# A layer stack of attention, feed-forward and Mamba-2 mixer on one core: the mixer's opening, the place of B and C, of the inner products and of the last weights

## The chip, the core and the metric

The kernel runs on one core of one Trainium2 chip. A core has five engines with a queue each, and each queue runs in order: TensorE (PE) for matmuls, VectorE (DVE), ScalarE (ACT), GpSimd (POOL), and SyncE (SP), which here only starts DMA transfers. The metric is the device time of one execution in microseconds; what is compared is the median of several executions.

## What is computed

Input x is 4 sequences of 256 tokens with 512 channels, all in float32. Four layers follow one another, each added to its input: attention with an adapter, a clustered feed-forward layer, the mixer (a Mamba-2 layer with 128 heads of 64, state size 128, 8 groups), and the feed-forward layer again. The change is in the mixer alone:

```python
x = x + attn_a(layernorm(x)); x = x + ffn(layernorm(x))
x = x + attn_b(layernorm(x)); x = x + ffn(layernorm(x))
# attn_b, the mixer:
proj = input_states @ in_proj_w.T
gate, xBC, dt = proj[..., :8192], proj[..., 8192:18432], proj[..., 18432:]
xBC = silu(causal_conv4(xBC) + conv_b)
hs, Bm, Cm = ...                        # x by head; B and C by group
dt = softplus(dt + dt_bias); dA = dt * A
y = ssd(hs, A, Bm, Cm, D, dt)           # sum over j <= i of (C_i.B_j) exp(sum of dA over j+1..i) dt_j x_j, plus D x
g = y * silu(gate)
gg = g.reshape(b, l, G, GS)             # normalised by group of 1024 channels
g = (gg * rsqrt(mean(gg * gg) + EPS)).reshape(b, l, INTER) * norm_w
return g @ out_w.T
```

## The kernel before

**Tiling.** Tokens lie in one row of 1024 (`NT`), in two halves of 512, in chunks of 64 (`Q`), or in eight tiles of 128 (`TT`). The 8192 inner channels are 64 blocks (`NB`) of 128 channels, two heads each; eight blocks (`GB`) are a group, which has one B and one C block of its own. Products in float32 precision are made by `mm3` (L110): both operands are split into an upper and a lower part and three matmuls are summed. So every weight is first cast (upper part, ACT) and then subtracted (lower part, DVE or POOL). `upper_piece(i)` (L821) makes the upper part of projection weight i and gives back a function that makes the lower part and fetches weight i+3; `upper_out(n)` (L1163) does it for an output weight, scaled by the norm weight.

**Projection.** `projected(kind, n)` (L1243) is a generator: the first `next` allocates a PSUM tile `pp` for 128 channels x 1024 tokens, each further one issues 12 matmuls for one half of the tokens. Two such tiles exist (`ps_p`); only the gate of block 0 lies in another place. A tile is free again when its last reader is done: for x, B and C the three `taps` on DVE (L1000), for a gate its Silu on ACT.

**A block i** (L1323) works with three generations of data: it projects x and gate of block i, and finishes block i-1:

- `decays(i-1)`: `exponentials` (L1073) on ACT for both heads, 7 activations each, on tiles `em` which `differences` (L1061, DVE) filled;
- `turn(i-1)`: 8 transposes `trx` on PE, multiplied by dt on DVE (L1102);
- `weigh(i-1)`: the `em` tiles times the masked scores `gm` of the group, on DVE (L1092);
- `conv` (ACT, L989) and `taps` (DVE) on x of block i, then `side_by_side` (Silu on ACT, L1015);
- `inner_products(i-1)`: 32 products `pyy` on PE (L1118, 64 records in the trace), then `gated` on DVE (L1125), which frees the PSUM of `pyy` and gives gb;
- `spilled` writes gb of block i-2 to DRAM, `squared` (L1143) adds its square to the group's `sq`: Square on ACT, addition on POOL (DVE for block 63);
- the gate's Silu `gts[i]` (L1442) at the end.

Beside this, from group 1 on, a block makes the output product `outer` of one token tile of the group before (24 matmuls `pog`); the gated values come back from DRAM by `recall` and are split by `upper_recalled` (L1205). B of the next group is projected at the end of a group's fourth block, C at the end of its fifth (`NEXT`), and the block after applies `conv`, `taps` and Silu to it. The seventh block of a group makes the next group's `scores` (L1024), in four parts `pg`, two PSUM tiles at a time.

**Opening.** The weights dt and B are projected before the mixer's block loop. `steps()` (L925) is a generator on dt: step 1 adds the bias; step 2 takes softplus by exp and log, with a polynomial e(1 - e/2 + e^2/3) where e is small; step 3 scales and makes cumulated sums of both halves (`tensor_tensor_scan`), stores them to DRAM (`cumd`), and step 4 transposes them (`trd`). `rows(h)` (L1048) loads a head's cumulated sums back, broadcast to 64 partitions, as `r`. `started()` (L1261) runs steps 1 to 3 around B and C, and blocks 0 and 1 follow as cases of `block`: block 0 runs step 4, block 1 makes the scores of group 0 between projection of x and turn.

**Order.** In the mixer's loop the order on PE, ACT, DVE and POOL is the program's (`tc.manual_schedule`, L1461); the order of SP's transfers and of what follows the loop is the scheduler's. In block 63 the last `outer` and four `upper_out` come, and `begin(0)`, `begin(1)`, `begin(2)`, which recall and split gated values of the last group, all ahead of the gate's Silu. After the loop (L1467 to L1486) come decays, turn and weigh of block 63, three half output products `begun`, the last inner products, and the sums of squares `pqs`; then the final loop over the eight token tiles (L1503) with output products, norm and feed-forward.

Of the kernel before, what the change touches and what calls it, by code (L numbers as in the profile page):

```python
# [20 lines left out]
P = 128  # L21
B, L, C = 4, 256, 512
NT = B * L
# [56 lines left out]
def hybrid_kernel(  # L80
# [705 lines left out]
    def mixer(feed, later):  # L786
        with ExitStack() as es, ExitStack() as inner:
# [137 lines left out]
            def steps():  # L925

                reset = p2.tile([P, NT], F32, name="reset", tag="sq", bufs=1)[:, :512]
# [7 lines left out]
                for e in es2:  # L935
                    nc.scalar.activation(e, e, AF.Exp)
                for e, lg in zip(es2, lgs):
                    nc.scalar.activation(lg, e, AF.Ln, bias=ones[:, 0:1])

                for s, e, engine in zip(ss, es2, (nc.vector, nc.gpsimd)):  # L940
                    engine.tensor_scalar(s, e, 1.0 / 3.0, -0.5, ALU.mult, ALU.add)
                    engine.tensor_tensor(s, s, e, ALU.mult)
                    engine.tensor_scalar(s, s, 1.0, None, ALU.add)
                    engine.tensor_tensor(s, s, e, ALU.mult)
# [20 lines left out]
                yield  # L965
# [7 lines left out]
                yield  # L973
# [169 lines left out]
            def squared(n, x2, gb):  # L1143

                g = n // GB
                if g not in sqs:
                    sqs[g] = p2.tile([P, NT], F32, name="sq", tag="sq", bufs=1)
                    nc.scalar.activation(sqs[g], gb, AF.Square)
                else:
                    nc.scalar.activation(x2, gb, AF.Square)  # L1150
                    (nc.gpsimd if n < NB - 1 else nc.vector).tensor_tensor(sqs[g], sqs[g], x2, ALU.add)  # L1151
# [6 lines left out]
            def fetch_out(n):  # L1158
                if n < NB:
                    wraws[n] = po_.tile([P, C], F32, name="wor", tag="wor", bufs=4)  # L1160
                    load(wraws[n], wout[n])

            def upper_out(n):  # L1163

                r = wraws.pop(n)
                w = [po_.tile([P, C], F32R, name=f"wo{j}", tag=f"wo{j}", bufs=GB) for j in range(2)]
                wos.setdefault(n // GB, []).append(w)
                nc.scalar.activation(w[0], r, AF.Copy, scale=nw_s[:, n : n + 1])

                def lower():  # L1170
                    nc.vector.scalar_tensor_tensor(
                        w[1], r, nw_s[:, n : n + 1], w[0].bitcast(F32), ALU.mult, ALU.subtract
                    )
                    if n % GB < 4:
                        fetch_out(n + 4)

                return lower
# [83 lines left out]
            def started():  # L1261

                prepare(2)
                next(dt_steps)
                pieces.pop(0)
                group["b"] = conv(first[1], NB, False)
                taps(group["b"], first[1], NB)
                next(dt_steps)
                prepare(3)
                fetch(6)  # L1270
                pp = whole(projected("c", 0))
                group["c"] = conv(pp, NB + G, False)
                silu(group["b"])
                next(dt_steps)
                taps(group["c"], pp, NB + G)
                rr.update((h, rows(h)) for h in range(2))

# [29 lines left out]

            def decays(i):
                for h, e in zip((2 * i, 2 * i + 1), ems[i]):
                    exponentials(h, e)  # L1310
# [8 lines left out]
            def inner_products(i):  # L1319
                py = product(xds.pop(i), ems.pop(i))  # L1320
                gbs[i] = gated(i, xs2[i], gts.pop(i), py)

            def block(i):  # L1323
# [33 lines left out]
                if i:  # L1357
                    decays(i - 1)
                waiting = [k for k in "bc" if k + "pp" in group]
                for k in waiting:  # L1360
                    group[k] = conv(group[k + "pp"], (NB if k == "b" else NB + G) + g + 1, False)
                if i == 1:
                    next(x_steps)
                    scoring = scores(group.pop("b"), group.pop("c"))
                    gms[0] = next(scoring)
                    for _ in scoring:
                        pass
                if i:
# [18 lines left out]
                if i == 0:  # L1387
                    pp = whole(g_steps)
                    next(dt_steps)
                    silu(group["c"])  # L1390
# [50 lines left out]
                gts[i] = p2.tile([P, NT], F32, name="gt", tag="gt", bufs=2)  # L1441
                nc.scalar.activation(gts[i], pp, AF.Silu)  # L1442
# [42 lines left out]
            rgs[G - 1] = root(sums(G - 1))  # L1485
            nc.vector.reciprocal(rgs[G - 1], rgs[G - 1])  # L1486
# [110 lines left out]
```

## Time and profile before

| | us |
|---|---|
| median of 3 executions (1876.27 to 1877.36) | 1876.93 |
| the profiled execution | 1875.91 |
| its span, first to last instruction | 1874.1 |
| PE busy | 1792.8 |
| DVE busy | 1428.6 |
| ACT busy | 1275.4 |
| POOL busy | 252.1 |

The mixer's normalisation begins at about 363 us, C's projection at 390 us; in block 7, the last of group 0, the Silu of x starts at 555.68 us; block 63 is under way at 1748 us, and the final loop runs from about 1800 us. An operation's row in the profile names line, engine, operation, output and inputs, and its duration. A number in brackets behind it is the time for which the engine stood idle before it, with what released it. The page also gives, in 40 slices of 46.9 us, the busy share of each engine and the clock granted to PE in tenths of full speed. Durations of PE are modelled and overlap: two matmuls of 512 columns that follow one another show 0.39 us each, and start 0.2275 us apart.

The larger transfers, with the engine that issues them and the median time from issue to landing:

```profile
wr<-in_win_dram SPq DMA_DIRECT2D x144, 256.0 KB, 2.7
r<-cumd SPq DMA_DIRECT2D x256, 128.0 KB, 2.9
gr<-spill SPq DMA_DIRECT2D x120, 256.0 KB, 3.3
wor<-in_wout_dram SPq DMA_DIRECT2D x64, 256.0 KB, 4.3
```

### The profile page before, as it was taken

The numbers are of one execution on the slowest core, as the hardware profiler recorded it, in microseconds if no ns is written. First come the engines' busy times: TensorE is split into PE (matmuls) and PEld (weight loads), VectorE is DVE, ScalarE is ACT, GpSimd is POOL, SyncE is SP. The second block draws the span as 40 slices with busy tenths as digits, with TensorE's granted clock in tenths as the row PEclk, the third lists the DMA queues.
The fourth block names the chain that finished last, engine by engine and source line by source line (L and its number), as shares of the span: only waits on it lengthen the run. The fifth ranks groups of instructions, "written<-read, shape, count | busy, mean of one in ns | idle before, by whom it ended". The sixth has DMA issues, their size and how long they took to land.

```text
span 1874.1 us, 33084 instructions
## 1 busy us (share of the span) xinstructions
PE 1792.8 (96%) x12882; PEld 1463.0 (78%) x12882; DVE 1428.6 (76%) x2156; ACT 1275.4 (68%) x2518; POOL 252.1 (13%) x255
## 2 busy tenths in 40 slices
PE   8999988889799999999999999999999999999997
PEld 6777767677677888888888888888888888888776
DVE  5576667777788787877787887879787878887776
ACT  6666675366678666766776677668676866777653
POOL 6332230010111011011110110111111011101100
PEclk9999989889999999999999999999999999999999
DMA  4000000112225332533343243224332532343321
GB/s 144 1 1 1 22 15 24 42 45 80 84 85 158 96 96 85 158 107 96 113 130 102 91 150 120 86 96 147 96 101 86 172 105 92 112 134 108 101 82 50
DMA packets 134237, 169.45 MB, mean 90 GB/s; under 512 B 12224, under 2 KB 77376, under 8 KB 134080
## 3 DMA queue, kind: packets, MB, share of 16 engines
q1 hardware_dynamic: 125008, 134.30, 23.6%
q10 hardware_dynamic: 9072, 33.03, 4.6%
q8 instruction: 101, 1.65, 0.3%
q14 instruction: 56, 0.46, 0.1%
HBM read 131.64 MB, written 35.65 MB: 89 GB/s over the span
## 4 chain that ended last, share of the span: by engine, by line
PE 80%; DVE 8%; ACT 7%; issue 2%; POOL 1%; DMA 1%; SPq 0%; DVEq 0%; ACTq 0%; POOLq 0%
PE pp L115 14%; PE pp L117 13%; PE pp L116 13%; PE pyy L1118 8%; PE pog L115 6%; PE pog L117 6%; PE pog L116 6%; PE trx L1099 3%; ACT e L477 2%; PE ptr L493 1%; PE pq L115 1%; PE pg L1036 1%; DVE acc L1006 1%; PE pq L116 1%; PE pq L117 1%
## 5 line engine op out<-in xcount | busy, mean ns | idle before, releaser
L115 PE MATMUL pp<-mx,w 128*128 128x512 f32 (+1 forms) x1160 | 468.2, 404 | 10.3 <-DVE bc L1006 9.8
L117 PE MATMUL pp<-mx,w 128*128 128x512 f32 (+1 forms) x1160 | 455.0, 392 | 1.9 <-DVE w L830 1.9
L116 PE MATMUL pp<-mx,w 128*128 128x512 f32 (+1 forms) x1160 | 454.8, 392 | 0.0
L1151 POOL TENSOR_TENSOR sq<-sq,x 128x1024 f32<-128x1024 f32 x55 | 132.0, 2399 | 1257.5 <-ACT x L1150 1257.5
L115 PEld LDWEIGHTS pp<-mx,w 128*128 128x128 f32 x1160 | 220.2, 190 | 56.8 <-issue 10.6
L117 PEld LDWEIGHTS pp<-mx,w 128*128 128x128 f32 x1160 | 220.2, 190 | 48.9 <-DVE w L830 2.6
L116 PEld LDWEIGHTS pp<-mx,w 128*128 128x128 f32 x1160 | 220.8, 190 | 40.7
L1006 DVE SCALAR_TENSOR_TENSOR acc<-pp,cw_s,acc 128x1012 f32<-128x1012 f32 (+2 forms) x192 | 244.6, 1274 | 7.2 <-ACT acc L995 2.6
L1092 DVE TENSOR_TENSOR em<-em,gm 128x1280 f32<-128x1280 f32 x128 | 188.7, 1489 | 70.8 <-ACT em L1087 70.8
L1102 DVE TENSOR_TENSOR xd<-trx,dt_t 128x512 f32<-128x512 f32 x128 | 82.5, 686 | 168.8 <-PE trx L1099 168.8
L115 PE MATMUL pog<-wo,gh 128*128 128x512 f32 x512 | 202.3, 395 | 2.3 <-ACT gh L1209 1.3
L117 PE MATMUL pog<-wo,gh 128*128 128x512 f32 x512 | 200.8, 392 | 0.8 <-DVE gh L1214 0.8
L116 PE MATMUL pog<-wo,gh 128*128 128x512 f32 x512 | 200.3, 392 | 0.0
L1018 ACT ACT_TABLE_LOAD x63 | 80.8, 1283 | 163.4 <-DVE acc L1006 163.3
L1442 ACT ACTIVATE gt<-pp 128x1024 f32<-128x1024 f32 x64 | 65.7, 1027 | 161.8 <-PE pp L117 161.8
L1118 PEld LDWEIGHTS pyy<-em,xd 64*64 64x64 f32 x4096 | 136.1, 136 | 50.7 <-issue 17.6
L1118 PE MATMUL pyy<-em,xd 64*64 64x256 f32 (+3 forms) x4096 | 164.6, 306 | 7.8 <-DVE em L1092 7.8
L1079 ACT ACTIVATE em<-r,end_t 128x128 f32<-128x128 f32 x512 | 163.0, 389 | 0.8
L477 ACT ACTIVATE e<-sc,nmx 128x256 f32<-128x256 f32 (+1 forms) x256 | 104.0, 441 | 21.0 <-DVE nmx L471 20.9
L115 PEld LDWEIGHTS pog<-wo,gh 128*128 128x128 f32 x512 | 96.8, 189 | 22.8 <-ACT gh L1209 1.8
L117 PEld LDWEIGHTS pog<-wo,gh 128*128 128x128 f32 x512 | 96.7, 189 | 21.4 <-DVE gh L1214 1.1
L116 PEld LDWEIGHTS pog<-wo,gh 128*128 128x128 f32 x512 | 96.8, 189 | 19.5
(298 smaller groups left out, 3191.3 us busy)
## 6 DMA issues: line engine op xcount, KB each, us to landing
wr<-in_win_dram SPq DMA_DIRECT2D x144, 256.0 KB, 2.7
r<-cumd SPq DMA_DIRECT2D x256, 128.0 KB, 2.9
spill<-gb ACTq DMA_DIRECT2D x63, 512.0 KB, 3.2
gr<-spill SPq DMA_DIRECT2D x120, 256.0 KB, 3.3
wor<-in_wout_dram SPq DMA_DIRECT2D x64, 256.0 KB, 4.3
out_dram<-x SPq DMA_DIRECT2D x8, 256.0 KB, 2.4
x<-in_x_dram SPq DMA_DIRECT2D x1, 1536.0 KB, 8.8
gr<-spill SPq DMA_DIRECT2D x8, 192.0 KB, 2.5
```

The costliest lines, as they stand in the source:

```text
L115: nc.tensor.matmul(o, lh, rh, start=(first and k == 0), stop=False)
L116: nc.tensor.matmul(o, lh, rl, start=False, stop=False)
L117: nc.tensor.matmul(o, ll, rh, start=False, stop=(last and k == n - 1))
L477: nc.scalar.activation(es_[c][:, 2 * j + pr, :], sc[:, j, :], AF.Exp, bias=nm[:, j : j + 1], accum_out=rs[:, c, h : h + 1],)
L1006: nc.vector.scalar_tensor_tensor(av[:, :, d:], pv[:, :, : L - d], cw_s[:, ch, tap : tap + 1], av[:, :, d:], ALU.mult, ALU.add,)
L1018: nc.scalar.activation(pair(x2).rearrange("p k u i -> p u k i"), acc.rearrange("p (u k i) -> p u k i", u=2, i=Q), AF.Silu,)
L1079: nc.scalar.activation(piece(e, j, c, 2 - c, 2), rv[:, j, 2:, :], AF.Exp, bias=end_t[:, 2 * j + c, h : h + 1],)
L1092: nc.vector.tensor_tensor(e, e, gm, ALU.mult)
L1102: nc.vector.tensor_tensor(xd[:, hs, :].rearrange("p c (h d) -> p c h d", h=2), tr.rearrange("p c (h d) -> p c h d", h=2), dt_t[:, hs, 2 * ...
L1118: nc.tensor.matmul(py[d, u, j * L + c * Q : (j + 1) * L].rearrange("p (k i) -> p k i", i=Q), xd[us, 4 * j + c, d], piece(es2[hh], j, c)[us ...
L1151: (nc.gpsimd if n < NB - 1 else nc.vector).tensor_tensor(sqs[g], sqs[g], x2, ALU.add)
L1442: nc.scalar.activation(gts[i], pp, AF.Silu)
```

## The change

It has five parts.

1. In `steps()` the polynomial is written as e((e/sqrt 3 - 0.75/sqrt 3)^2 + 13/16): a Square on ACT and one operation on DVE for each half of the tokens. Steps 3 and 4 are cut: each half of the cumulated sums, and each of the three transposed quantities, is a step of its own.
2. `started()` and blocks 0 and 1 become `opening()`, an order of its own; the loop over `block` begins at 2.
3. In group 0 the block after B's (or C's) projection runs its `conv` and `taps` ahead of `decays(i-1)`. In later groups the order stays: conv, turn, weigh, taps.
4. In blocks that make no output product (2 to 8, and the second block of each later group) `inner_products(i-1)` moves behind the second half of the gate's projection. In the seventh block of group 0 the first scores stay between the gate's halves.
5. The end: the output weights 61 to 63 are loaded into the tiles of projection weights; in block 63 `begin(0)` comes first, the weights 56 to 59 and 61 to 63 are split, and `begin(1)` comes, all ahead of the gate's Silu, while `begin(2)` and weight 60 come after `weigh(63)`. The square of block 62 is added on DVE. The second half of the first token tile's output product and the sums come inside the ordered part.

```diff
-                reset = p2.tile([P, NT], F32, name="reset", tag="sq", bufs=1)[:, :512]
+                reset = p2.tile([P, NT], F32, name="reset", tag="sq", bufs=1)
+                shift3 = reset[:, 512:513]
+                reset = reset[:, :512]
+                nc.gpsimd.memset(shift3, -0.75 * float(np.sqrt(1.0 / 3.0)))
                 nc.gpsimd.memset(reset, 1.0)
...
+                for e, s in zip(es2, ss):
+                    nc.scalar.activation(s, e, AF.Square, bias=shift3, scale=float(np.sqrt(1.0 / 3.0)))
                 for e, lg in zip(es2, lgs):
                     nc.scalar.activation(lg, e, AF.Ln, bias=ones[:, 0:1])
-                for s, e, engine in zip(ss, es2, (nc.vector, nc.gpsimd)):
-                    engine.tensor_scalar(s, e, 1.0 / 3.0, -0.5, ALU.mult, ALU.add)
-                    engine.tensor_tensor(s, s, e, ALU.mult)
-                    engine.tensor_scalar(s, s, 1.0, None, ALU.add)
-                    engine.tensor_tensor(s, s, e, ALU.mult)
+                for e, s in zip(es2, ss):
+                    nc.vector.scalar_tensor_tensor(s, s, 13.0 / 16.0, e, ALU.add, ALU.mult)
                 yield
...
-                    (nc.gpsimd if n < NB - 1 else nc.vector).tensor_tensor(sqs[g], sqs[g], x2, ALU.add)
+                    (nc.gpsimd if n < NB - 2 else nc.vector).tensor_tensor(sqs[g], sqs[g], x2, ALU.add)
...
-                    wraws[n] = po_.tile([P, C], F32, name="wor", tag="wor", bufs=4)
+                    wraws[n] = (
+                        po_.tile([P, C], F32, name="wor", tag="wor", bufs=4) if n < NB - 3
+                        else pw.tile([P, C], F32, name="wor2", tag="wr", bufs=3)
+                    )
...
-                    if n % GB < 4:
+                    if n % GB < 4 and n + 4 < NB - 3:
...
-            def started():
...
+            def gate(i, pp):
+                gts[i] = p2.tile([P, NT], F32, name="gt", tag="gt", bufs=2)
+                nc.scalar.activation(gts[i], pp, AF.Silu)
...
+            def opening():
...
-                pp = whole(projected("c", 0))
-                group["c"] = conv(pp, NB + G, False)
+                c = whole(projected("c", 0))
+                group["c"] = conv(c, NB + G, False)
+                lower = upper_piece(4)
                 silu(group["b"])
                 next(dt_steps)
-                taps(group["c"], pp, NB + G)
+                x0 = whole(projected("x", 0))
+                acc0 = conv(x0, 0, True)
+                taps(group["c"], c, NB + G)
+                lower()
+                lower = upper_piece(5)
+                silu(group["c"])
+                g0 = whole(projected("g", 0))
+                gate(0, g0)
+                next(dt_steps)
                 rr.update((h, rows(h)) for h in range(2))
...
+                x_steps = projected("x", 1)
+                next(x_steps)
+                next(x_steps)
+                taps(acc0, x0, 0)
+                lower()
+                next(dt_steps)
+                lower = upper_piece(6)
+                next(dt_steps)
+                ems[0] = [differences(h) for h in range(2)]
+                x1 = next(x_steps)
+                xs2[0] = side_by_side(acc0)
+                next(dt_steps)
+                scoring = scores(group.pop("b"), group.pop("c"))
+                gms[0] = next(scoring)
+                next(scoring)
+                next(scoring)
+                g_steps = projected("g", 1)
+                next(g_steps)
+                next(g_steps)
+                decays(0)
+                for _ in scoring:
+                    pass
+                lower()
+                lower = upper_piece(7)
+                turn(0)
+                weigh(0)
+                g1 = next(g_steps)
+                acc = conv(x1, 1, True)
+                taps(acc, x1, 1)
+                inner_products(0)
+                xs2[1] = side_by_side(acc)
+                lower()
+                ems[1] = [differences(h) for h in (2, 3)]
+                gate(1, g1)
...
-                if i:
-                    decays(i - 1)
                 waiting = [k for k in "bc" if k + "pp" in group]
-                for k in waiting:
+                def begun_next(k):
                     group[k] = conv(group[k + "pp"], (NB if k == "b" else NB + G) + g + 1, False)
-                if i == 1:
-                    next(x_steps)
-                    scoring = scores(group.pop("b"), group.pop("c"))
-                    gms[0] = next(scoring)
-                    for _ in scoring:
-                        pass
-                if i:
-                    turn(i - 1)
-                    weigh(i - 1)
-                for k in waiting:
+                def ended_next(k):
                     taps(group[k], group.pop(k + "pp"), (NB if k == "b" else NB + G) + g + 1)
-                if i != 1:
-                    next(x_steps)
+                for k in waiting if g == 0 else ():
+                    begun_next(k)
+                    ended_next(k)
+                decays(i - 1)
+                for k in waiting if g else ():
+                    begun_next(k)
+                turn(i - 1)
+                weigh(i - 1)
+                for k in waiting if g else ():
+                    ended_next(k)
+                next(x_steps)
                 acc = conv(pp, i, True)
...
-                if i == 0:
-                    pp = whole(g_steps)
-                    next(dt_steps)
-                    silu(group["c"])
...
-                if i:
-                    next(g_steps)
-                    if not done:
-                        pp = next(g_steps)
-                    if i == 1:
-                        next(g_steps)
+                scoring = None
+                def scored():
+                    nonlocal scoring
+                    if gi == 6 and g + 1 < G:
+                        scoring = scores(group.pop("b"), group.pop("c"))
+                        gms[g + 1] = next(scoring)
+                        next(scoring)
+                        next(scoring)
+                next(g_steps)
+                if done or both:
                     inner_products(i - 1)
                     if both:
                         done = outer(G - 2, TT - 1)
-                    if done:
-                        pp = next(g_steps)
-                scoring = None
-                if gi == 6 and g + 1 < G:
-                    scoring = scores(group.pop("b"), group.pop("c"))
-                    gms[g + 1] = next(scoring)
-                    next(scoring)
-                    next(scoring)
-                if i > 1:
+                    pp = next(g_steps)
+                    scored()
                     next(g_steps)
+                else:
+                    pp = next(g_steps)
+                    scored()
+                    next(g_steps)
+                    inner_products(i - 1)
...
                 if both:
+                    for k in range(3):
+                        fetch_out(NB - 3 + k)
+                    begin(0)
+                    lower.extend(upper_out(g * GB + k) for k in range(4))
                     scaled(*done)
-                    for k in range(4):
-                        upper_out(g * GB + k)()
-                    begin(0)
+                    lowered()
+                    lower.extend(upper_out(g * GB + k) for k in range(5, GB))
                     begin(1)
-                    begin(2)
+                    lowered()
...
-                gts[i] = p2.tile([P, NT], F32, name="gt", tag="gt", bufs=2)
-                nc.scalar.activation(gts[i], pp, AF.Silu)
+                gate(i, pp)
...
-                started()
-                for i in range(NB):
+                opening()
+                for i in range(2, NB):
...
                 weigh(i)
+                begin(2)
+                upper_out(i - 3)()
+                wos[G - 1].insert(4, wos[G - 1].pop())
                 for t in range(3):
                     begun(t)
                 begin(3)
-                lower = [upper_out(i - 3 + k) for k in range(4)]
                 squared(i - 1, xs2.pop(i - 1), gbs.pop(i - 1))
                 inner_products(i)
-                for f in lower:
-                    f()
                 spilled(i, gbs[i])
+                begun(3)
+                partial(pos[0], G - 1, parts(G - 1, 0, 1), 1)
                 squared(i, xs2.pop(i), gbs.pop(i))
-                begun(3)
-            rgs[G - 1] = root(sums(G - 1))
-            nc.vector.reciprocal(rgs[G - 1], rgs[G - 1])
+                rgs[G - 1] = root(sums(G - 1))
+                nc.vector.reciprocal(rgs[G - 1], rgs[G - 1])
...
-                partial(po, G - 1, parts(G - 1, t, 1), 1)
+                if t:
+                    partial(po, G - 1, parts(G - 1, t, 1), 1)
```

More of the change, by code (lines that the diff above doesn't have):

```diff
@@ L964, in steps @@
                     )
-                yield
+                    yield
                 for v, n, end, func in ((cums, 4, col_t, AF.Copy), (suf, 2, end_t, AF.Copy), (dts, 4, dt_t, AF.Relu)):
@@ L972, in steps @@
                         nc.scalar.activation(end[:, n * j : n * j + n, :], tr, func)
-                yield
+                    yield
             def piece(v, j, c, k=0, n=None):
@@ L1260, in mixer @@
             sqs, wos, rgs, gms, group, rr = {}, {}, {}, {}, {}, {}
-            def started():
-                prepare(2)
-                next(dt_steps)
[L1265 to L1270, printed above, removed]
-                pp = whole(projected("c", 0))
-                group["c"] = conv(pp, NB + G, False)
-                silu(group["b"])
-                next(dt_steps)
-                taps(group["c"], pp, NB + G)
-                rr.update((h, rows(h)) for h in range(2))
             dt_steps = steps()
@@ L1321, in inner_products @@
                 gbs[i] = gated(i, xs2[i], gts.pop(i), py)
+            def opening():
+                prepare(2)
+                next(dt_steps)
+                pieces.pop(0)
+                group["b"] = conv(first[1], NB, False)
+                taps(group["b"], first[1], NB)
+                next(dt_steps)
+                prepare(3)
+                fetch(6)
+                c = whole(projected("c", 0))
+                group["c"] = conv(c, NB + G, False)
+                lower = upper_piece(4)
+                silu(group["b"])
+                next(dt_steps)
[8 more added lines that the diff above has]
+                next(dt_steps)
+                rr.update((h, rows(h)) for h in range(2))
+                x_steps = projected("x", 1)
[3 more added lines that the diff above has]
+                lower()
+                next(dt_steps)
+                lower = upper_piece(6)
+                next(dt_steps)
+                ems[0] = [differences(h) for h in range(2)]
+                x1 = next(x_steps)
+                xs2[0] = side_by_side(acc0)
+                next(dt_steps)
+                scoring = scores(group.pop("b"), group.pop("c"))
[20 more added lines that the diff above has]
+                gate(1, g1)
             def block(i):
@@ L1386, in block @@
                 g_steps = projected("g", i)
-                if i == 0:
-                    pp = whole(g_steps)
-                    next(dt_steps)
-                    silu(group["c"])
                 xs2[i] = side_by_side(acc)
```

## The prediction, made before the changed kernel was built or run

> **What bounds the kernel now.** I read first the page's slices, then the busy times by stage, then who TensorE (PE) waits for, then the order in time at the waits.
>
> ```profile
> PE   8999988889799999999999999999999999999997
> PEclk9999989889999999999999999999999999999999
> ```
>
> The only dips inside the mixer (which begins in slice 8) are in slices 8 to 12, and the clock dips with them. The stages:
>
> ```profile
> core 0: us, PE busy (x) PEld busy (x) DVE busy (x) ACT busy (x) POOL busy (x), PEclk, DMA share, GB/s
> 388.30:452.60 64.30, 55.40 (x365) 44.24 (x363) 52.66 (x65) 42.37 (x68) 8.39 (x8) 0.89 0.21 66
> 467.40:522.40 55.00, 45.18 (x291) 35.59 (x288) 37.60 (x43) 34.22 (x53) 5.25 (x3) 0.88 0.23 77
> 577.00:594.40 17.40, 13.55 (x102) 10.94 (x100) 15.32 (x20) 16.97 (x29) 2.38 (x1) 0.80 0.61 169
> 594.40:1766.00 1171.60, 1171.60 (x8390) 961.86 (x8389) 936.96 (x1185) 839.87 (x1399) 113.01 (x47) 1.00 0.36 112
> 1766.00:1800.00 34.00, 28.77 (x180) 22.74 (x178) 22.33 (x32) 17.97 (x34) 2.46 (x2) 0.95 0.36 113
> ```
>
> From 594 to 1766 PE is busy without a hole, at clock 1.00: nothing done to the other engines there can save more than tenths. All that can be won lies before 594 and after 1766. Who PE waits for from 388 to 600:
>
> ```profile
> PE pp L115 <- DVE bc L1006: 9.8, 2, 4.9
> PE pyy L1118 <- DVE em L1092: 5.8, 3, 2.0
> PE trd L971 <- ACT dcum L958: 2.4, 1, 2.4
> PE pp L117 <- DVE w L830: 1.9, 1, 1.9
> PE pg L1036 <- DVE gm L1043: 1.6, 2, 1.1
> ```
>
> How much is lost before 594.36, where the first `pqs` starts? From 388.3 PE does 563 projection matmuls (0.2275 us from start to start), 20 dt transposes (2.2), two sets of scores (2 x 2.6), nine turns (9 x 0.85) and nine inner products (9 x 2.36): 164.4 us. It takes 206.1. So 41.7 us are holes and half-clock stretches. In the tail the holes from 1775 to 1800 are 5.2 us and the slow matmuls around them about 3.7.
>
> **A. Group 0, blocks 4 and 5 (B and C ahead of decays).** Now the gate's projection waits for the PSUM that the next group's B (then C) holds until its `taps`, which stand on VectorE (DVE) behind `weigh(i-1)`:
>
> ```profile
> 487.08 0.77 PE L115 MATMUL pp<-mx,w 128*128 128x512 f32 x1 [4.91 <-DVE bc L1006]
> ```
>
> The wait is 4.91 us, and the 12 matmuls behind it take 5.46 instead of 2.73. The same at 514.68: 15.3 us in both. The change puts `conv` and `taps` of B or C ahead of `decays`. The stall goes; what is late next? I follow the mark S(i), the Silu of `side_by_side` in block i. ScalarE (ACT) and DVE have a loop from one to the next: load and Silu 2.3, cast 0.55, gate 1.05, load and 14 exponentials 6.65 (559.52 to 566.2), second `weigh` 1.5, three taps 3.9: 15.95, and S(7) to S(8) is 555.68 to 571.67, 15.99. PE's own work is 14.1 per block. So group 0 runs by this loop, not by PE. S(3) = 468.87 to S(8) takes 102.8 now. After the change:
> - S(3) to S(4): B's projection may start at S(3) (PSUM of x3), ends 5.5 later; conv 1.2 (ACT idles 1 us, since it reached this point at 4.5); decays 6.65, weigh 1.5, taps 3.9: 18.7, now 21.9. The DVE taps of B (6.7 to 10.5) and the turn end before the first weigh can start.
> - S(4) to S(5): Silu of B adds 1; C's projection starts 0.9 after S(4): 19.6, now 27.6.
> - S(5) to S(6): Silu of C adds 1: 16.9, now 20.3.
> - S(6) to S(7): the second pair of scores now stands behind the inner products and waits for masks that DVE makes only after S(6): 17.3, now 17.0. Scores behind the first gate half cost nothing: that is where they stood.
> - S(7) to S(8): 16.0, unchanged.
>
> Sum 88.5, a gain of 14.3. I take **13**, for the reason in B.
>
> **B. Inner products behind the whole gate.** 12 matmuls (2.73 us) move ahead of `pyy` in blocks 2 to 8 and in every second block of a group (9, 17, ... 57). `gated` on DVE, and behind it `differences`, the lower halves of weights, the next turn and weigh, wait for `pyy`. In group 0 `pyy` would end 1.5 us before S(i), and `gated` stands behind the taps that end at S(i): covered. In block 17 `pyy` would end at 768.3, and DVE reaches `gated` only at 771.08: cover of 2.8 us. In blocks 17 to 57 PE also loses 0.4 us now inside `pyy` (2.81 at 763.15, otherwise 2.41) for the second `weigh`; that goes: 6 x 0.4 = **2.4**. In block 9 the waits of 1.84 and 2.01 and the slow matmuls behind (4.54 for 2.3) go: S(9) stays 19.0 behind S(8), as ACT's eight `wo` scalings still stand there, but `pqs` starts about S(9), now 3.65 behind S(9): **4**.
>
> [...] In group 0 PE will idle 1.5 to 3 us in each block. A row on this:
>
> ```profile
> 446.19 0.61 PE L1118 MATMUL pyy<-em,xd 64*64 64x256 f32 x2
> 448.76 3.92 PE L1118 MATMUL pyy<-em,xd 64*64 64x256 f32 x62 [1.96 <-DVE em L1092]
> ```
>
> After a hole of 1.96 us, 62 matmuls take 3.92 us (64 take 2.41 at 434.46). [...] By the row each hole of about 2 us may cost 1.6 more; the holes of 1.06 and 0.96 cost nothing. In most blocks PE has 2 us to spare against the loop, but B's and C's projections lie on it: up to 1.6 twice. I go by the row and take off 1.3.
>
> **C. Opening.** Mark S(1), now 436.64. Now all of the cumulated decays stand on DVE (399.4 to 409.0) ahead of C's taps, so x of block 1 starts its second half at 417.29, behind the 1.93 wait of L830. After the change, on DVE from the end of B's taps, 395.34: the polynomial is two operations of 0.69 instead of four (395.26 to 399.49), with two Squares on ACT (an Exp of that shape is 0.62; a Square after Exp at 448.18 shows no table load) and none on POOL: 396.7. First half of the decays (0.42+0.76+0.69+0.49+1.23+0.42 = 4.0) 400.7; taps of C 404.6; lower piece 0.7, 405.3; second half 409.3; taps of x0 413.2; lower 413.9; differences 2.2, but their rows r come two DMAs after the second `cumd` store (408.59 now, read by 415.8): 417.5. PE runs on to 406.9 as now, then x of block 1 at once; transposes (col copies at 411.6, end 413, dt 416.4), first scores 417.1, gate half, scores 421.1, turn 422.2. DVE masks to 421.7, lower 422.3, xd 423.6, weigh twice 426.4 (ACT: decays from 416.4, done 423.1), taps of x1 3.9: S(1) = 430.3. That is **6.3** earlier; S(2) and S(3) keep the distance. The `cumd` stores and `r` loads go out as early as now on SP, and the weight fetches behind them earlier, because the lower pieces come earlier. I take **6**, between 2 (rows or PSUM turns late by 4) and 8.
>
> **D. Tail.**
>
> ```profile
> 1775.34 0.62 ACT L1209 CAST gh<-gr 128x512 fp32r<-128x512 f32 x1 [9.15 <-DMA gr<-spill]
> 1775.87 1.02 ACT L1442 ACTIVATE gt<-pp 128x1024 f32<-128x1024 f32 x1
> ```
>
> The last gate stands on ACT behind `begin(2)`, whose recalled half waits for a buffer and for SP, which has four `wor` loads ahead of it. The change puts `begin(2)` behind `weigh(63)`; ACT gets three more `wo` scalings (0.65 each) and then takes the gate when its projection ends, 1772.2, instead of 1775.87. The three weights load into free `wr` buffers without waiting. Decays end 1779.9 and weigh 1781.4, 3.7 earlier. But `begun(2)` stands on PE ahead of the inner products, and its cast is now behind the decays (1780.5), its lower behind weigh (1782.1): PE idles from 1778.5, a new hole of 3.5 us with a half clock behind it. `pyy` ends 1787 to 1790 (now 1788.5). Behind it much is better: weights 4 to 7 are split already, the half of pos[0] runs before the sums, the square of block 62 is added on DVE (1.22; POOL 2.37 while a DVE operation of 0.69 took 2.49 beside it). With `pyy` ending at 1788.5, sums end 8.0 later (begun 2.7, pos[0] 3.6, sums 1.7), and `scaled(0)` starts at 1797.2, now 1800.54: 3.3; PE's place in its work is 7 better, which the chain of the first tile cannot all use. **4**, between 0 and 8.
>
> **Sum.** 13 + 4 + 2.4 + 6 + 4 = 29.4 from the profiled execution's own time (1875.91, span 1874.1): 1846.5. The median shown is 1.0 above it (1876.93): **1848**.
>
> **Rivals.**
> - Half of it (1864): the half clock stays on in group 0, 1.6 us in each of eight blocks (13), and the tail gives nothing (4). For: the row of B and the new hole in D. Against: PE has some 2 us per block in hand. 12%.
> - Only the stalls of blocks 4 and 5 and block 9 go (1857): the opening stays at 436 since r or PSUM turns of the transposes hold DVE, tail 1. For: new waits of 1.5 to 3 us that I can't see. 13%.
> - Slower: `pyy` behind the whole gate drags DVE. Place: blocks 9, 17 to 57. If `gated` were reached before `pyy` ends, each us would pass through differences and weigh to the next `pyy`, with a half clock of about 2 behind the hole. It decides from 2.8 us of slip on, and must reach about 5 us in seven blocks (35) to eat the 29: 1882. Against: the DVE row at 771.08. 4%.
> - The change doesn't do what it says: B's conv waits for its projection on ACT and decays come as late as the stall was; no change, 1876. 3%.
>
> The forecast keeps 68%. A measurement of this kernel can tell about 0.2% from no change. Range: low end all bounds good (14.3+5+2.4+8+8 = 38), 1839; high end 1865, which takes in the first two rivals.
>
> **What would show it.** Right: no wait of `pp` on `bc` L1006; S(3) to S(8) near 89; S(1) near 430; `pqs` of group 0 near 571; blocks 17 to 57 with `pyy` of 2.41; last gate at its projection's end and a hole before `begun(2)`. Wrong: PEclk under 1 through slices 9 to 12, a DVE wait on `pyy` in blocks 17 to 57, or DVE waiting for `r` in the opening.

## The result, and the profile after

| | before | after |
|---|---|---|
| median, us (4 executions each) | 1876.60 (1874.50 to 1877.36) | 1849.58 (1848.57 to 1851.47) |
| ratio, 95% interval | | 0.9859 (0.9842 to 0.9876) |
| span of the profiled execution | 1874.1 | 1848.1 |
| from the opening's start to the end | 1484.45 | 1458.10 |

The last row is the one to compare by. The layers before the mixer have the same code in all kernels of this study, yet the first `de` operation on VectorE (DVE), where the mixer's opening starts, lies anywhere from 386.1 to 393.2 us in twelve traces. So stages are counted from `de` below: 26.35 us are won. The page of the changed kernel, in the lines that answer to those shown before (the same 40 slices):

```profile
PE   7999989899999999999999999999999999999997
PEclk9999999999999999999999999999999999999999
```

The dips of slices 9 to 12, of PE and of its clock, are gone; slice 8, where PE still shows an 8, ends at 370 us, ahead of the opening. Who PE waits for from 388 to 580 us (us in all, times, longest):

```profile
PE pp L115 <- DVE acc L1008: 5.1, 4, 1.5
PE pyy L1120 <- DVE em L1094: 2.4, 2, 1.9
PE trx L1101 <- DVE gm L1045: 2.2, 2, 1.7
PE pg L1038 <- DVE gm L1045: 1.6, 1, 1.6
```

`bc`, 9.8 us before, is no longer among them, nor `w`. In its place stands `acc`: PE now runs ahead and waits for the taps of x, that is for the loop of ScalarE (ACT) and DVE (not in blocks 4 and 5, see below). The stages, with busy times and the granted clock:

```profile
core 0: us, PE busy (x) PEld busy (x) DVE busy (x) ACT busy (x) POOL busy (x), PEclk, DMA share, GB/s
390.00:431.80 41.80, 37.37 (x246) 29.57 (x244) 36.80 (x48) 29.82 (x46) 2.85 (x5) 1.00 0.22 70
463.20:553.40 90.20, 85.80 (x680) 69.60 (x680) 78.52 (x97) 70.29 (x116) 11.95 (x5) 1.00 0.30 97
553.40:572.50 19.10, 17.03 (x121) 13.49 (x121) 16.97 (x22) 18.98 (x33) 2.37 (x1) 0.91 0.54 166
572.50:1747.70 1175.20, 1175.20 (x8420) 964.07 (x8418) 947.27 (x1201) 845.37 (x1406) 113.36 (x48) 1.00 0.36 113
1747.70:1775.00 27.30, 22.91 (x151) 17.42 (x150) 15.64 (x23) 16.39 (x32) 0.00 (x0) 0.87 0.36 110
```

Blocks 4 to 8 (second row) take 90.2 us at full clock; two places below full clock are left before 1775 us, in block 9 and in the tail. By marks, each from the trace (S(i) is the start of the Silu of block i, behind its table load):

| way | before | after | won |
|---|---|---|---|
| opening to S(3) | 80.51 | 74.50 | 6.0 |
| S(3) to S(8) | 102.80 | 90.18 | 12.6 |
| S(8) to S(9) | 19.04 | 19.05 | 0.0 |
| S(9) to the first `pqs` | 2.36 | -1.28 | 3.6 |
| first `pqs` to the last turn | 1177.84 | 1175.18 | 2.7 |
| last turn to the end | 101.90 | 100.47 | 1.4 |

### The profile page after: what moved, and what is told of

Read it like the earlier page. It is cut to its first block, busy times and chain, and to the rows that moved or that the text cites. A ratio compares the mean times of both kernels' runs of the same rounds, so it can differ in the third digit from the quotient of the medians.

```text
span 1848.1 us, 33082 instructions
## 1 busy us (share of the span) xinstructions
PE 1777.1 (96%) x12882; PEld 1448.5 (78%) x12882; DVE 1425.8 (77%) x2155; ACT 1276.9 (69%) x2520; POOL 245.0 (13%) x251
## 3 DMA queue, kind: packets, MB, share of 16 engines
q1 hardware_dynamic: 125008, 134.30, 23.9%
## 4 chain that ended last, share of the span: by engine, by line
PE 80%; DVE 8%; ACT 7%; issue 2%; POOL 2%; DMA 1%; SPq 0%; ACTq 0%; DVEq 0%; POOLq 0%
PE pp L115 13%; PE pp L116 13%; PE pp L117 13%; PE pyy L1120 7%; PE pog L115 6%; PE pog L117 6%; PE pog L116 6%; PE trx L1101 3%; ACT e L477 2%; PE ptr L493 1%; DVE acc L1008 1%; PE pq L115 1%; ACT em L1081 1%; PE pg L1038 1%; PE pq L116 1%
## 5 line engine op out<-in xcount | busy, mean ns | idle before, releaser
L1120 PEld LDWEIGHTS pyy<-em,xd 64*64 64x64 f32 x4096 | 129.5, 134 | 44.6 <-issue 18.4
L1120 PE MATMUL pyy<-em,xd 64*64 64x256 f32 (+3 forms) x4096 | 157.6, 302 | 2.4 <-DVE em L1094 2.4
```

The lines of the kernel that those rows point to most:

```text
L1120: nc.tensor.matmul(py[d, u, j * L + c * Q : (j + 1) * L].rearrange("p (k i) -> p k i", i=Q), xd[us, 4 * j + c, d], piece(es2[hh], j, c)[us ...
```

## The experiments

Times below are medians of four executions, where no other number is given. Because of the drift ahead of the mixer, the length from `de` to the end in one profiled execution is given too (changed kernel: 1458.10). Marks come from that one execution of each kernel.

**1. B and C behind the decays again.**

```diff
-                for k in waiting if g == 0 else ():
+                for k in ():
...
-                for k in waiting if g else ():
+                for k in waiting:
```

> The changed kernel with part 3 undone: in group 0, too, decays come ahead of conv of B and C, and weigh ahead of their taps. My theory: the stall of the gate's projection behind the taps returns in blocks 4 and 5 (a hole near 4.9 us each, half clock behind it), so the mark from block 3 to block 6 (55.95 us in the changed kernel, 69.85 before) takes 64 to 70 us, and the whole is 8 to 14 us slower than the changed kernel: 1858 to 1864. Rival: with the whole gate ahead of the inner products the place of B and C no longer matters; 0 to 2 us, no hole over 2 us in blocks 4 and 5.

Measured: 1866.66, from `de` 1474.32: 16.2 longer. Who PE waits for, from 388 to 590 us of this kernel:

```profile
PE pp L115 <- DVE bc L1008: 9.8, 2, 4.9
PE pp L115 <- DVE acc L1008: 5.1, 4, 1.5
```

The two holes of 4.9 us are back beside those of the changed kernel. S(3) to S(6) takes 68.6 us (55.95), as expected; the rival falls. It is more than 14 us in all because a half-clock stretch in block 9 happens to be 10.2 us long here (3.4 in the changed kernel): the 16 matmuls of the first sums (`pqs`) take 3.57 us and the 24 output matmuls behind them 7.77, instead of 1.95 and 5.71.

**2. Inner products between the gate's halves again.**

```diff
                     pp = next(g_steps)
+                    inner_products(i - 1)
                     scored()
                     next(g_steps)
-                    inner_products(i - 1)
```

> The changed kernel with part 4 undone: the inner products stand again between the halves of the gate's projection. My theory: slower by 4 to 7 us (1854 to 1857): in block 9 the waits inside the inner products return (about 4), blocks 17 to 57 lose 0.4 each (2.4), and against that the spill of block 6, which in the changed kernel holds ScalarE for 1.27 us ahead of the decays of block 7, no longer waits. Rival: the move costs on VectorE and ScalarE what it saves on TensorE: within 1 us of the changed kernel, 1848 to 1851.

Measured: 1853.32, from `de` 1464.20: 6.1 longer, and the rival falls. `pyy` waits for `em` six times and 8.8 us in all from 388 to 575 (two and 2.4 in the changed kernel):

```profile
PE pyy L1120 <- DVE em L1094: 8.8, 6, 2.0
```

S(9) to the first `pqs` is 2.53 (-1.28); S(7) to S(8) is 15.97 (17.62), so the new wait in block 8, which run 4 takes away, does belong to this part.

**3. The old polynomial.**

```diff
-                for e, s in zip(es2, ss):
-                    nc.scalar.activation(s, e, AF.Square, bias=shift3, scale=float(np.sqrt(1.0 / 3.0)))
...
-                for e, s in zip(es2, ss):
-                    nc.vector.scalar_tensor_tensor(s, s, 13.0 / 16.0, e, ALU.add, ALU.mult)
+                for s, e, engine in zip(ss, es2, (nc.vector, nc.gpsimd)):
+                    engine.tensor_scalar(s, e, 1.0 / 3.0, -0.5, ALU.mult, ALU.add)
+                    engine.tensor_tensor(s, s, e, ALU.mult)
+                    engine.tensor_scalar(s, s, 1.0, None, ALU.add)
+                    engine.tensor_tensor(s, s, e, ALU.mult)
```

> The changed kernel with the old polynomial, four operations for each half, one half on VectorE and one on GpSimd, and no Squares on ScalarE. My theory: the chain of the opening is VectorE's, so its 2.7 us more (and slower operations beside GpSimd) arrive at the Silu of block 1 in full: that mark 3 to 4 us later and the whole 3 to 4 us slower, 1852 to 1854. Rival: the reordering alone makes the opening; the mark of block 1 moves by less than 1 us, 1849 to 1851.

Measured: S(1) at 46.22 from `de` (43.11), 3.1 later, and the end 3.4 later; the median, 1851.44, is only 1.9 above the changed kernel's, with a `de` 1.5 us earlier. The opening is a chain on DVE, and what is taken off it arrives in full: the two polynomials differ by 3.0 us on DVE (1.28 us in the changed kernel, 4.25 here).

**4. Two more moves**, against two waits that the trace of the changed kernel shows. The first, in block 8's run-up, on ACT:

```profile
538.55 1.02 ACT L1299 ACTIVATE gt<-pp 128x1024 f32<-128x1024 f32 x1
540.84 0.33 ACTq L1141 DMA_DIRECT2D spill<-gb  x1
541.25 1.28 ACT L1081 ACT_TABLE_LOAD   x1 [1.69 <-DVE gb L1135]
```

The spill of gb is a transfer that ACT issues, ahead of the decays in its queue. Since the inner products moved, gb is later, and the decays wait behind the issue though they need nothing of gb. The second is the hole ahead of the third half product in the tail:

```profile
1756.18 0.69 PE L115 MATMUL pog<-wo,gh 128*128 128x512 f32 x1 [2.04 <-ACT gh L1215]
1756.67 0.63 PE L116 MATMUL pog<-wo,gh 128*128 128x512 f32 x1
1757.80 0.79 PE L117 MATMUL pog<-wo,gh 128*128 128x512 f32 x1 [0.50 <-DVE gh L1220]
1758.39 0.63 PE L115 MATMUL pog<-wo,gh 128*128 128x512 f32 x1
1758.82 0.63 PE L116 MATMUL pog<-wo,gh 128*128 128x512 f32 x1
```

Starts lie 0.43 us apart behind it, not 0.2275: half clock (PEclk 0.50 from 1757.8 to 1762.3).

```diff
-                if i >= 2:
+                if i > GB:
                     spilled(i - 2, gbs[i - 2])
...
                 decays(i - 1)
+                if i <= GB:
+                    spilled(i - 2, gbs[i - 2])
...
-                decays(i)
                 turn(i)
-                weigh(i)
+                exponentials(2 * i, ems[i][0])
+                weighted(ems[i][0], gms[G - 1])
                 begin(2)
+                exponentials(2 * i + 1, ems[i][1])
+                weighted(ems[i][1], gms[G - 1])
```

> The changed kernel with two more moves: up to block 8 the spill is issued on ScalarE behind the decays instead of ahead of them, and in the tail the recalled half of token tile 2 is split between the decays of the two last heads instead of behind both. My theory: the 1.27 us wait ahead of the decays of block 7 goes, and the mark from block 7 to block 8 is 16.3 instead of 17.6; the hole of 2.0 us ahead of the third half product in the tail falls under 1 us and with it the half clock; the end comes 3 to 5 us earlier: 1845 to 1847. Rival: what is won in the tail is lost again in the final loop, whose chain from the first scaled tile sets the end: 1848 to 1849.

Measured: 1843.71, ratio to the kernel before 0.9831 (0.9817 to 0.9846), from `de` 1451.61: 6.5 shorter than the changed kernel. S(7) to S(8) is 15.95. In the tail the hole has shrunk and the clock is whole:

```profile
1753.13 0.39 PE L116 MATMUL pog<-wo,gh 128*128 128x512 f32 x1
1754.07 0.50 PE L117 MATMUL pog<-wo,gh 128*128 128x512 f32 x1 [0.55 <-DVE gh L1220]
1754.40 0.40 PE L115 MATMUL pog<-wo,gh 128*128 128x512 f32 x1
1754.64 0.39 PE L116 MATMUL pog<-wo,gh 128*128 128x512 f32 x1
```

From the last turn to the end it takes 95.25 us (100.47): the hole and the half clock behind it were worth 5.2 in these two executions, and the final loop hands all of it on. The rival falls.

**5. The hole in block 9 filled**, on top of run 4.

```diff
                     next(g_steps)
+                    if i == GB + 1:
+                        warmed(ps.tile([P, C], F32, name="warm", tag="m"), [x[:, t, :] for t in range(2)])
                     inner_products(i - 1)
```

> The kernel with the two more moves, and in block 9 two matmuls of 512 columns in plain float32 (about 0.85 us each, their result is not used) ahead of the inner products, where TensorE has a hole of 1.59 and then one of 0.63 us. My theory: a hole of that size is what brings the half clock found behind it (3.4 us in that kernel; 3.4, 6.8 and 10.2 behind holes of 1.93 to 2.01 at the same place in others); with it filled the clock stays whole and the way from the first to the second sums of squares is 173.9 us instead of 175.5; 1 to 2 us faster than that kernel, 1842. [...]

Measured: 1843.77, first to second sums 175.55, as in run 4, where holes of 1.59 and 0.63 us stand in block 9 and half clock behind them. My theory falls: the hole inside `pyy` is filled, and the half clock is there.

```profile
567.30 1.88 PE L122 MATMUL warm<-x,ones 128*128 128x512 f32 x4
569.11 2.94 PE L1120 MATMUL pyy<-em,xd 64*64 64x256 f32 x64
572.67 1.95 PE L1190 MATMUL pqs<-ones,sq 128*128 128x1 f32 x16 [0.62 <-POOL sq L1153]
574.47 0.65 PE L115 MATMUL pog<-wo,gh 128*128 128x512 f32 x1
574.92 0.63 PE L116 MATMUL pog<-wo,gh 128*128 128x512 f32 x1
```

The only hole left is 0.62 us, ahead of the sums; and what stands around it is narrow work, `pyy` with 64*64 where the output matmuls have 128*128, and sums of one column (128x1).

**6. Block 8's weights scaled early**, on top of run 4: ACT does it while it waits for the taps.

```diff
+                early = [upper_out(k) for k in range(4)] if i == GB else []
                 xs2[i] = side_by_side(acc)
...
-                    lower.extend(upper_out((g - 1) * GB + k) for k in range(4))
+                    lower.extend(early or [upper_out((g - 1) * GB + k) for k in range(4)])
```

> The kernel with the two more moves, and block 8 scales its four output weights on ScalarE while that waits for the taps, ahead of the Silu of x, instead of between it and the gate. My theory: group 0 runs by the loop of ScalarE and VectorE up to block 9, so the mark from block 8 to block 9 falls from 19.06 to 16.4 us, the hole in block 9 goes and the half clock with it: 2 to 4 us faster than that kernel, 1840 to 1842. Rival: VectorE, which still makes the lower halves at the old place, or TensorE sets the time there: less than 1 us.

Measured: 1840.15 (1837.77 to 1845.41), ratio to the kernel before 0.982 (0.980 to 0.984). S(8) to S(9) is 17.29 (19.06; forecast 16.4), the first `pqs` 2.4 earlier, no hole and no half clock in block 9, though a hole of 1.26 us in the turn of block 10; by the last turn the lead over run 4 is 2.5. Of it 1.5 are lost again in the tail, where this execution has a half-clock stretch of 3.4 us that run 4's has not. It is the fastest version by median; that it beats run 4 is not certain, as the intervals overlap.

**7. The old opening with the short polynomial.** `started()` and the cases for blocks 0 and 1 are put back, with the cut steps taken two and three at a time:

```diff
-                opening()
-                for i in range(2, NB):
+                started()
+                for i in range(NB):
```

> The changed kernel with part 2 undone: the old opening and blocks 0 and 1 as cases of the block, but with the short polynomial. My theory: of the 5 to 6 us won in the opening the polynomial makes 3.4 (as the run with the old polynomial shows) and the order only the rest, so from the first operation of the opening on VectorE the Silu of block 1 is 2 to 3 us later than in the changed kernel (43.1), and the whole 2 to 3 us slower, 1851.5 to 1852.5. Rival: the order makes all of it, and without it the short polynomial buys nothing: 5 to 6 us slower, 1855 to 1856.

Measured: S(1) at 44.90 (43.11) and S(3) at 76.80 (74.50), so 1.8 to 2.3 later; the rival's 5 to 6 is not there. The median, 1856.07 (1850.51 to 1857.99), looks like the rival's number. In the profiled execution, the slowest of the four, it is not its doing: 2.9 of the 5.2 us from `de` to the end arise in the tail, whose code is unchanged, where a second half-clock stretch of 6.8 us stands.

**8. The old tail.** Part 5 undone: one `wor` ring, `begin(2)` ahead of the gate, weights 4 to 7 split behind the last inner products, the sums behind the ordered part.

```diff
-                begin(2)
-                upper_out(i - 3)()
-                wos[G - 1].insert(4, wos[G - 1].pop())
...
+                lower = [upper_out(i - 3 + k) for k in range(4)]
```

> The changed kernel with part 5 undone: the old tail. My theory: from the last turn to the end 101.9 us as before, 1.4 more than in the changed kernel (100.5), since the new hole ahead of the third half product and the half clock behind it eat most of the gain: 1851. Rival: the tail's worth is the 4 us that were forecast and the rest is lost elsewhere: 1853.5.

Measured: 101.94 from the last turn to the end, 1.5 more than in the changed kernel, as expected. But one execution says little here: of six traces with the changed kernel's tail, five take 99.67 to 100.93 us and one (run 7) 103.36. The median, 1849.44, can't tell it from the changed kernel.

**9 and 10. Both holes filled; the hole of the changed kernel filled** (one execution each). Run 9 is run 5 with one more such matmul behind `inner_products`; run 10 is the changed kernel with three ahead of them.

> The kernel with the two more moves and both holes of block 9 filled: two float32 matmuls ahead of the inner products, as in the run with the filler, and one more (0.85 us) between them and the sums of squares, where 0.62 us were empty and the 24 output matmuls behind the sums took 7.31 us (5.71 at full clock). Theory A: what brings the half clock is a stretch in which TensorE does little, the narrow inner products, a hole and the sums of one column each, though no hole in it reaches 1 us: with the second hole filled the 24 matmuls take 5.7 us and the way from the first to the second sums is 174.0 us. Theory B: the holes have nothing to do with it: 7.3 and 175.5 stay.

> The changed kernel itself, where the hole of 1.93 us lies inside the inner products of block 9 and 62 of their records behind it take 4.05 us (2.34 at full clock), with three float32 matmuls ahead of them to fill it. Theory A: the inner products run at full clock, but VectorE's and GpSimd's square still comes no earlier, a hole of about 0.5 us is left ahead of the sums, and the half clock moves behind it: first sums near 181.5 us after the opening's start (182.45 in the changed kernel), 24 output matmuls behind them in 7.3 us, 175.5 from the first to the second sums; nothing is won. Theory B: with the hole the half clock goes: first sums near 181.5, 173.9 from first to second, 1 us won.

Run 9: no half clock; the 24 matmuls take 5.69 us, first to second sums 174.46, near what theory A said. Run 10: a hole of 0.61 us is left ahead of the sums, just as in run 5, and the 24 matmuls behind take 5.72: no half clock, so A fails here. B's microsecond is not won either: first sums 0.96 earlier (181.49), and 0.84 lost again until the second (174.77), with a new hole of 0.58 in the turn of block 10; from `de` 1458.04.

These two do not show that the filler keeps the clock whole, for run 8 has block 9 as in the changed kernel, nothing filled, and no half clock there. First the changed kernel, then run 8:

```profile
568.49 4.05 PE L1120 MATMUL pyy<-em,xd 64*64 64x256 f32 x62 [1.93 <-DVE em L1094]
```

```profile
567.21 2.40 PE L1120 MATMUL pyy<-em,xd 64*64 64x256 f32 x62 [1.94 <-DVE em L1094]
570.24 1.95 PE L1187 MATMUL pqs<-ones,sq 128*128 128x1 f32 x16 [0.62 <-POOL sq L1153]
```

The same 62 products behind the same hole take 4.05 us in one and 2.40 in the other. Run 8's first sums (181.45) and its way to the second (174.76) are those of run 10, so the filler of run 10 won nothing that run 8 has not. What decides is not shown by these runs; a count over the traces follows in the last section.

## Why the prediction was right

The forecast was 1848 with a gain of 29.4 on the profiled execution; 26.35 were won from the opening's start on, and the medians differ by 27.0. Point by point:

- **A, blocks 4 and 5** (13): S(3) to S(8) gave 12.6, and run 1 puts the two holes back. The steps forecast as 18.7, 19.6, 16.9, 17.3 and 16.0 are 19.3, 19.8, 16.9, 16.6 and 17.6. For the last three steps the loop of ACT and DVE was the right bound. For the first two, where the gain was made, "by this loop, not by PE" does not hold after the change. From S(3) to S(5) PE has no hole (the number behind the times is the length of the stretch, the next PE's busy time):

```profile
464.52:483.80 19.28, 19.28 (x144) 15.83 (x143) 17.63 (x20) 14.70 (x24) 2.39 (x1) 1.00 0.29 96
483.80:503.58 19.78, 19.78 (x146) 16.24 (x145) 17.93 (x21) 15.65 (x25) 2.40 (x1) 1.00 0.34 107
```

A block's 14.1 us of PE work and the 5.5 of B or C make 19.6, an estimate from the forecast's own starts, and the steps are about that long: PE's own work, which the forecast did not hold against these two steps, is as near a bound as the loop. The last step holds a wait that I had not seen: I listed who stands behind `gated` on DVE, but not the spill's issue, which waits for gb on ACT ahead of the decays (1.7; runs 2 and 4). That the sum fits 13 is partly luck: I had taken 1.3 off for half clock, and there was none.
- **The row, and the half clock.** The forecast let PE idle 1.5 to 3 us in each block of group 0, and took 1.3 off for it by the row at 448.76. PE idled 0 to 1.7, and PEclk stayed 1.00 from 431.8 to 553.4. No hole there was as long as the row's 1.96 us, so the row was not put to the test, and no run shows the 1.3 taken off by it. Elsewhere half clock did follow holes of 1.93 and 2.04 us (changed kernel, block 9 and tail), of 1.95 and 2.01 in other traces, and once a hole of 0.62 (run 5); and in run 8 it did not follow one of 1.94. For holes of up to 2.04 us, the length alone does not tell in these traces whether half clock follows.
- **B, inner products behind the whole gate**: block 9 gave 3.6 (forecast 4), and blocks 9 to 62 gave 2.7 (2.4); run 2 shows both. The cover on DVE held: between 572.5 and 1747.7 PE is busy throughout.
- **C, opening** (6): 5.2 at S(1), forecast 6.3, and 6.0 at S(3). Of the 1.1 missing, 0.9 is one DVE operation of the first half's decays, which took 1.40 us and stood in the sum as 0.49. DVE did wait for `r`, a sign that I had named for being wrong, but only 0.4 us. Undone alone, the polynomial costs 3.1 at S(1) and the order 1.8 there and 2.3 at S(3).
- **D, tail** (4): 1.4. This is the term that was mis-sized. The new hole came as described, with 2.04 and 0.50 us where I gave 3.5, and a half clock of 6.8 us behind it. But `pyy` ended near the late end of what I gave, so that from the last turn to the tail's sums 23.8 us passed (24.8 before), and the lead of 2.6 us at the first tile's transposes (1778.89, turn at 1747.65; before 1806.02 and 1772.20) shrank to 1.4 in the final loop. Runs 4 to 6, with the hole mostly gone, take 5.2, 3.7 and 3.7 less from the last turn on. By the scatter given under run 8, the 1.4 itself is not certain.

No rival came true. The nearest, half clock in group 0 and nothing from the tail, failed by its first premise, while its second came near; VectorE was never held by `pyy` in blocks 17 to 57, where `pyy` takes 2.41 us throughout. The first `pqs` came at 572.5 (forecast 571).

## What to carry to other kernels

Find out which loop of queues sets a stage before costing what moves in it: here PE had up to 1.7 us in hand in most blocks of group 0, and none in the two with B and C, so what counted were the operations that stood on ACT and DVE ahead of the next release. In block 8's run-up the spill, a transfer issued from ACT's queue, waited for gb and held the decays behind it for 1.69 us; when the source of such a transfer moves later, move the issue as well. Runs that differ by a few us are better compared by marks within the trace than by medians, when other parts of the program drift by as much.

## What was not expected of the hardware

The same instructions ahead of the mixer took 386.1 to 393.2 us, of which 23.9 to 41.0 us passed at half clock (37.5 in the kernel before, 34.1 in the changed kernel). Stretches of half clock in the tail, not counting one that runs past the last instruction (from 1841.65 us in the changed kernel), came and went between kernels with the same tail code or nearly: one of 6.8 us in the changed kernel (100.47 us from the last turn to the end), two of 6.8 in run 7 (103.36), and, with the two halves of the last gate weighted one at a time, one of 3.4 in runs 5 and 6 (96.8 each) and none in run 4 (95.25). Half clock (PEclk 0.50, so in the kernel before from 410.96 to 421.20 us) otherwise lasted 3.4, 6.8 or 10.2 us at a time, and within it matmuls of 512 columns started 0.43 us apart instead of 0.2275 (the changed kernel, from 1758.39 us).

A count over the twelve traces tells more than the length of holes. In each trace the starts of all half-clock stretches lie whole multiples of 3.413 us apart (17 stretches in the kernel before, 11 in the changed kernel, all within 0.02 us), and how this grid lies against the work differs from trace to trace. Cut by its grid, the twelve traces have 4907 intervals at full clock from 383 us to 60 us before the end. In each I add up the time in which PE was idle or made the one-column sums `pqs`. All 18 intervals with more than 2.05 us of it were followed by half clock, none with less than 1.72 us was, and in between there are 11 that were and others that were not. In the kernel before, five with 2.15 to 3.41 us were, and so were those with 1.94 and 1.72; in the changed kernel those with 2.04 and 1.92 were, and those with 1.77 and 1.74 were not.

So the grid parts run 8's hole of 1.94 us into 1.55 and 0.39, while 1.92 of the changed kernel's 1.93 fall into one interval (from 565.07 us). In run 5 the hole of 0.62 us shares an interval with 1.81 us of the sums; in run 10 the interval of the 0.61 holds only 0.28 us of them. That idle time within one interval decides fits all of this, but no run moved the grid on purpose, so it is not shown as the cause.
